# The end of a two-layer attention kernel: another division, norms by halves, two stores

## The chip, the cores and the metric

The kernel runs on one core of one Trainium2 chip. A core has a matrix engine (TensorE, PE in the profile), a vector engine (VectorE, DVE), a scalar engine (ScalarE, ACT), a general engine (GpSimd, POOL) and SyncE (SP), which here issues all transfers (DMAs). Each engine takes its instructions strictly in the order in which the program issues them to it, and engines wait for each other by semaphores. On-chip memory (SBUF) has 128 partitions, which are the rows of a tile; TensorE writes to a small memory of its own (PSUM). DRAM lies outside.

The metric is the device time in microseconds (us) of one execution; less is better.

## What is computed

Two layers of attention over x of 2048 rows and 256 columns, with 16 heads of 16 columns each. Layer 0 modulates, attends within and across the two halves of x, and ends with a GELU MLP. Layer 1 is cut below to what matters here; `memory` is a context of 1601 rows.

```python
def _layernorm(x, g, b):
    mu = jnp.mean(x, axis=-1, keepdims=True)
    var = jnp.var(x, axis=-1, keepdims=True)
    return (x - mu) * jax.lax.rsqrt(var + EPS) * g + b

x = tgt + _mha(tgt, tgt, tgt, ..., tgt_mask)      # stage 2, masked
x = _layernorm(x, g1, be1)
x = x + _mha(x, memory, memory, ..., None)        # stage 3
x = _layernorm(x, g2, be2)
x = x + (jax.nn.relu(x @ w1 + b1) @ w2 + b2)
x = _layernorm(x, g3, be3)
```

Within `_mha` the softmax over keys is followed by the product with the values, and the heads' outputs, side by side, by the projection `out @ ow + ob`.

## The kernel before

The 2048 rows are cut into four blocks of 512 (`BLK`), the 16 heads into four groups of four. A *unit* is one block and one group in one of four attention stages (0 and 1 of layer 0, 2 and 3 of layer 1). `stream` (L1197) runs all units one after another. For a unit TensorE makes the scores (L1035, L1042, masked ones L1050 too), ScalarE their exponentials (L1055), TensorE the product with the values into `u["av"]` (L1072). The scores of the next unit are made once more beforehand (L957) for their maxima. Between these steps the rest of the work is woven in by hand: generators in `background` that `advance` moves one step at a time, and `later`, a list of functions with a due step. A generator is a *chain*: what one block needs after its last group, namely projection, norm, MLP, and the next stage's queries, keys and values. Because the schedule is manual, the order in the program is the order on each engine.

A value matrix carries a column of ones, so that `u["av"]` holds for each head of the group, on 32 partitions each, 16 rows of sums and one row with the sum of the weights (row `ONE` = 16). The division of a unit is three functions:

- `copy_sums` (L1091): ScalarE copies `u["av"]` to `sums` (L1104). Four DMAs (L1110) spread the four rows of weights as 128x16 over all partitions, `weights`. Four more (L1119) bring the sums to the block's tile `oT`, where the heads lie without gaps: 64 rows for a group.
- `invert` (L1133): VectorE's reciprocal of the 128x16 weights (L1136). `to_rows` writes it to DRAM (L1141) and fetches it from there, each head's row copied to 16 partitions (L1143), into `rd_rows`.
- `divide` (L1146): GpSimd multiplies the 64x512 rows of `oT` by `rd_rows` (L1150).

For all units but the last, `invert` comes 3 and `divide` 6 steps after `copy_sums`, beside the next unit. After the last unit nothing is left to stand beside: `stream` runs what is pending, then the three functions in a row (L1336 to L1339), and then the last block's chain to its end.

That chain is `chain_last` (L745):

- `residual` loads t, the block's rows so far, 128x4x256 (L180). The tile has one buffer.
- `project` (L498) multiplies `oT` by the output weights in two halves of two row tiles each (L507); 256 columns of a tile are one row tile. `biased` (L530) takes each half: VectorE adds the bias row into u (L537), GpSimd adds u to t (L539).
- `post_norm` (L543): `normalize` runs VectorE's bn_stats (L366) and bn_aggr (L369) for all four row tiles, adds eps (L371), GpSimd raises to -1/2 (L372), VectorE applies mean and factor to each row tile (L375). GpSimd then multiplies by the row g and adds the row b, in two halves each, 128x512 (L550).
- `transposed` (L381): TensorE turns t (L390) by columns: all four row tiles of the first 128 columns, then of the second. ScalarE copies the first to `hT` (L405), VectorE the second (L407).
- `mlp` (L553): eight products up (L565) with ReLU on ScalarE (L574), then down in two halves (L618), each given to `biased` again.
- `post_norm` again, and one DMA of the block to `out` (L755).

A step that fills a PSUM bank is a `piece` (L118); its later functions, such as the copy out of the bank, are run when the chain moves on. SP's queue holds in its last part the division's DMAs, then the load of t, then the store.

Of the kernel before, what the change touches and what calls it, by code (L numbers as in the profile page):

```python
# [12 lines left out]
F32 = mybir.dt.float32  # L13
# [3 lines left out]
AF = mybir.ActivationFunctionType  # L17
ALU = mybir.AluOpType
# [4 lines left out]
P = 128  # L23
D = 256
H = 16
HD = 16
# [4 lines left out]
BLK = 512  # L31
NB = S // BLK
TPB = BLK // P
# [4 lines left out]
PH = 32  # L38
ONE = HD
# [37 lines left out]
def two_layers(ctx: ExitStack, tc: tile.TileContext, a: dict, out: bass.AP):  # L77
    nc = tc.nc

    def pool(name, bufs=1, **kw):  # L80
        return ctx.enter_context(tc.tile_pool(name=name, bufs=bufs, **kw))
# [7 lines left out]
    sb = pool("sb")  # L89
# [28 lines left out]
    def piece(*steps):  # L118

        yield BANK  # L120
        if streaming[0]:
            n = small[0]
            m = one_ps(n=n)
        else:
            n = None
            while len([e for e in unfinished if e[0] is None]) > 2:
                flush_one()
            m = ps.tile([P, 2, BLK], F32, tag="s", bufs=3, name="s_ps")[:, 0, :]
        left = [lambda f=f: f(m) for f in steps[1:]]
        entry = (n, left)  # L130
        unfinished.append(entry)
        steps[0](m)
        while left:

            yield 1 if len(left) > 1 else 0
            if left:
                left.pop(0)()
        if entry in unfinished:
            unfinished.remove(entry)

    def flush_one():
# [37 lines left out]
    def load_x(t, src):  # L179
        nc.sync.dma_start(t, src)  # L180
# [4 lines left out]
    def along(row, n=TPB, parts=P):  # L185
        return row.unsqueeze(1).to_broadcast([parts, n, D])
# [4 lines left out]
    def half(shape, dtype=F32, name="half"):  # L191
        return sb.tile(shape, dtype, tag="half", bufs=3, name=name)
# [76 lines left out]
    for g in range(NG):  # L269
        for i in range(2):  # L270
            at = (2 * g + i) * HD
# [19 lines left out]
    m = one_ps()  # L291
# [40 lines left out]
    m = one_ps()  # L332
# [165 lines left out]
    def project(st, b, finish):  # L498

        oT, wp = blocks[st, b]["oT"], outputs[st]  # L500

        def product(m, n):
            y = m.rearrange("p (t d) -> p t d", d=D)
            for q2 in range(2):
                qt = 2 * n + q2
                for k in range(2):
                    nc.tensor.matmul(  # L507
                        y[:, q2, :], lhsT=oT[:, k, qt * P : (qt + 1) * P],
                        rhs=wp[:, k, :], start=k == 0, stop=k == 1,
                    )  # L510

        for n in range(2):
            yield from piece(
                lambda m, n=n: product(m, n),
                lambda m, n=n: finish(n, m.rearrange("p (t d) -> p t d", d=D)),
            )
        done.add(("project", st, b))
# [111 lines left out]
    def residual(src):  # L629
        t = sb.tile([P, TPB, D], F32, tag="t", name="t")  # L630
        load_x(t, src)
        return t
# [112 lines left out]
    def chain_last(b):  # L745
# [8 lines left out]
        yield from post_norm(rows["m1"], t)  # L754
        nc.sync.dma_start(out[b * BLK : (b + 1) * BLK, :].rearrange("(t p) d -> p t d", p=P), t)  # L755

    chains = (chain_self, chain_cross, chain_masked, chain_last)
    blocks: dict = {}
    background: list = []
# [19 lines left out]
    def ensure(what):  # L779

        while what not in done:
            if not advance(background[0]):
                background.pop(0)
# [7 lines left out]
    def want(*place):  # L791
        waiting.extend((kind, *place) for kind in ("keys", "values"))
# [225 lines left out]
    def part_tile(u, name):  # L1018
        return sb.tile([P, 4 * BLK // P], F32, tag=f"{name}{u['g']}{u['part']}", name=name)
# [71 lines left out]
    def copy_sums(u):  # L1091


        st, b, g = u["st"], u["b"], u["g"]
        first_part = u.get("part") == 0
        if g == 0 and not first_part:
            before = ORDER[st].index(b)
            if before:
                ensure(("project", st, ORDER[st][before - 1]))
            elif st:  # L1100
                ensure(("project", st - 1, ORDER[st - 1][-1]))
            blocks[st, b]["oT"] = sb.tile([P, 2, BLK], F32, tag="oT", name="oT")
        sums = half([P, BLK], name="sums")
        nc.scalar.copy(sums, u["av"])  # L1104
        if "part" in u:
            u["weights"] = part_tile(u, "weights")
        else:
            u["weights"] = sb.tile([P, 4 * BLK // P], F32, tag="rd", bufs=4, name="weights")
        for j in range(4):
            nc.sync.dma_start(  # L1110
                u["weights"][PH * j : PH * (j + 1), :], sums[PH * j + ONE : PH * j + ONE + 1, :]
            )
        at = (g % 2) * (P // 2)
        if first_part:
            dst = first_sums[g] = dr.tile([P // 2, BLK], F32, tag="o", bufs=NG, name="o_dr")
        else:
            dst = blocks[st, b]["oT"][at : at + P // 2, g // 2, :]
        for j in range(4):
            nc.sync.dma_start(dst[HD * j : HD * (j + 1), :], sums[PH * j : PH * j + HD, :])  # L1119

        if st < 3 and b in (ORDER[st][-1], ORDER[st][1]):
            for slot in u["slots"]:
                if (st == 1 and slot == 1 and g in (1, 2)) or (st == 2 and b != ORDER[st][-1]):
                    continue
                want(st + 1, g, slot)
        if st == 1 and b == ORDER[1][-1] and g == 1:
            mask_part(0)
        if first_part and g == NG - 1:
            want(2, 2, 1)
# [3 lines left out]
    def invert(u):  # L1133

        rd = sb.tile([P, 4 * BLK // P], F32, tag="rd", bufs=4, name="rd")
        nc.vector.reciprocal(rd, u["weights"])  # L1136
        u["rd"] = to_rows(u, rd, sb.tile([P, BLK], F32, tag="rd_rows", name="rd_rows"))

    def to_rows(u, rd, dst):
        d = dr.tile([4, BLK], F32, tag="rd", bufs=4, name="rd_dr")  # L1140
        nc.sync.dma_start(d.rearrange("j (p c) -> (j p) c", p=PH), rd)  # L1141
        at = (u["g"] % 2) * (P // 2)
        nc.sync.dma_start(dst[at : at + P // 2, :], d.unsqueeze(1).to_broadcast([4, HD, BLK]))  # L1143
        return dst[at : at + P // 2, :]

    def divide(u):  # L1146
        g = u["g"]
        at = (g % 2) * (P // 2)
        v = blocks[u["st"], u["b"]]["oT"][at : at + P // 2, g // 2, :]
        nc.gpsimd.tensor_tensor(v, v, u["rd"], ALU.mult)  # L1150
        if u.get("part") == 1:
            rows_, sums = u["rd_first"], u["first"]
            nc.gpsimd.tensor_tensor(sums, sums, rows_, ALU.mult)
            nc.gpsimd.tensor_tensor(v, v, sums, ALU.add)
# [24 lines left out]
    def fetch_first(u):  # L1179
# [4 lines left out]
        nc.sync.dma_start(t[at : at + P // 2, :], first_sums[u["g"]])  # L1184
        u["first"] = t[at : at + P // 2, :]

    def chain_after(u):

        go = now[0] + (9 if "part" in u else 8)

        def gen():
            yield max(0, go - now[0])
            yield from chains[u["st"]](u["b"])

        background.append([gen(), 0, False])

    def stream(stages):  # L1197

        units = []
# [16 lines left out]
        at = 0  # L1216
# [69 lines left out]
        for u in units:  # L1286
            i = u["i"]
# [3 lines left out]
            for s2 in range(len(second)):  # L1291
# [22 lines left out]
                if s2 == 2 and i:  # L1314
                    w = units[i - 1]
# [10 lines left out]
                    if w["g"] == NG - 1 and part != 0:  # L1326
                        chain_after(w)
        small[0] = len(units) % 2
        for f in pending:
            if f:  # L1330
                f()
# [1 line left out]
            x[1]()  # L1333
        flush((0, 1))
        streaming[0] = False
        w = units[-1]  # L1336
        copy_sums(w)
        invert(w)
        divide(w)  # L1339
        chain_after(w)  # L1340
        while background:
            if not advance(background[0]):
                background.pop(0)
# [109 lines left out]
```

## Time and profile before

| | us |
|---|---|
| median of 3 runs | 3333.31 |
| lowest and highest run | 3326.55, 3346.01 |
| the profiled execution, its time | 3340.76 |
| its span, first to last instruction | 3338.9 |
| busy in the span: PE | 3054.3 |
| DVE | 2164.9 |
| ACT | 1718.1 |
| POOL | 404.0 |
| mean granted clock of PE | 0.969 |

The profile is of one execution, not of a median one: what is worked out from its rows stands against 3340.76. The profile has a page and can be asked for views. In the page, the span is cut into 40 slices with a digit for the busy tenths of each engine. The chain of waits starts at the last instruction and goes back: each piece is what released the next. "PE s_ps L507 x14" is 14 TensorE instructions of line 507 that write `s_ps`; "SPq" and "POOLq" are the engine's own queue work; "DMA rd_rows<-rd_dr" is the time from a transfer's issue until it was seen to have landed. In the timeline a row gives start, duration, engine, line, operation, shapes, and in brackets how long the engine had been idle and what ended that. A granted clock of 1.00 is full speed of PE, 0.50 half.

A product in 32 bits is two instructions on PE, so the eight products of `project`, four for each half, are the 16 instructions of L507.

### The profile page before, as it was taken

The page shows a single profiled execution, that of the slowest core. Times are in us where ns is not written, and L with a number is a line of the kernel's source. Part 1 is how long each engine was busy: PE and PEld are TensorE (multiplying, and loading weights), DVE is VectorE, ACT ScalarE, POOL GpSimd, SP SyncE. Part 2 cuts the span into 40 slices and gives each one's busy share as a digit, 9 for nine tenths or more (in the row PEclk, how much of TensorE's full clock was granted, in tenths as well). Part 3 has the DMA queues.
Part 4 walks back from the last instruction along what each step waited for, and adds up shares of the span by engine and source line. Part 5 has one row for each costly group of instructions (what it writes and reads, how often), then busy time and mean ns, then how long its engine had stood idle before and what let it go on. Part 6 is the DMA issues. An engine that isn't in the chain of part 4 may idle for free.

```text
span 3338.9 us, 56839 instructions
## 1 busy us (share of the span) xinstructions
PE 3054.3 (91%) x22592; PEld 1371.8 (41%) x22592; DVE 2164.9 (65%) x3925; ACT 1718.1 (51%) x1892; POOL 404.0 (12%) x344
## 2 busy tenths in 40 slices
PE   5889999999998989898999999999989999999995
PEld 2434444444444435343433343343344444444433
DVE  4666777775656566566777777777667757666541
ACT  1455565565555545443545555555556546545461
POOL 0001101101011122113013013010010010110102
PEclk8899999999999999999999999999999999999997
DMA  6462251260216121343012011003230100001000
GB/s 171 131 118 80 63 98 58 72 114 26 66 33 116 31 79 42 95 117 101 27 39 59 20 39 52 13 22 70 49 87 27 27 17 21 26 17 27 11 14 16
DMA packets 162363, 191.21 MB, mean 57 GB/s; under 512 B 82584, under 2 KB 95520, under 8 KB 162096
## 3 DMA queue, kind: packets, MB, share of 16 engines
q1 hardware_dynamic: 162096, 187.57, 22.8%
q8 instruction: 178, 2.92, 0.4%
q14 instruction: 89, 0.73, 0.1%
HBM read 129.91 MB, written 48.46 MB: 53 GB/s over the span
## 4 chain that ended last, share of the span: by engine, by line
PE 59%; DVE 6%; ACT 4%; DMA 3%; SPq 2%; issue 2%; POOL 1%; ACTq 0%; POOLq 0%; DVEq 0%
PE m_ps L1072 15%; PE s_ps L1035 10%; PE s_ps L957 9%; PE s_ps L1050 7%; PE s_ps L1042 6%; ACT e L1055 3%; PE m_ps L565 3%; PE m_ps L618 3%; DVE s_ps L965 2%; DVE pm L972 1%; PE m_ps L507 1%; PE m_ps L432 1%; DMA kT<-k_dr 1%; PE m_ps L462 1%; DVE t L375 1%
## 5 line engine op out<-in xcount | busy, mean ns | idle before, releaser
L1055 ACT ACTIVATE e<-s_ps 128x1024 f32<-128x1024 f32 (+1 forms) x1440 | 1466.9, 1024 | 1330.7 <-PE s_ps L1042 739.4
L972 DVE TENSOR_REDUCE pm<-s_ps 128x2 f32<-128x1024 f32 (+3 forms) x1024 | 1122.5, 1107 | 512.2 <-PE s_ps L957 508.9
L1072 PE MATMUL m_ps<-e,V 128*32 128x256 f32 (+2 forms) x10432 | 909.7, 420 | 1.0 <-DVE lo L440 0.8
L965 DVE CUSTOM_DVE_ANT_0 s_ps<-s_ps,bias 128x512 f32<-128x512 f32 x1024 | 713.2, 701 | 286.7 <-PE s_ps L957 147.4
L957 PE MATMUL s_ps<-kT,q 64*128 64x512 f32 (+3 forms) x3072 | 655.5, 428 | 112.4 <-ACT e L1055 63.9
L1035 PE MATMUL s_ps<-q,kT 64*128 64x512 f32 (+1 forms) x2880 | 681.6, 469 | 45.0 <-ACT e L1055 24.7
L1042 PE MATMUL s_ps<-nm,sel 64*128 64x512 f32 (+1 forms) x2880 | 576.2, 395 | 0.0
L957 PEld LDWEIGHTS s_ps<-kT,q 64*128 64x128 f32 x3072 | 295.4, 187 | 475.2 <-issue 244.1
L1035 PEld LDWEIGHTS s_ps<-q,kT 64*128 64x128 f32 (+1 forms) x2880 | 271.5, 185 | 506.9 <-issue 286.6
L1072 PEld LDWEIGHTS m_ps<-e,V 128*32 128x32 f32 (+1 forms) x10432 | 207.2, 109 | 442.6 <-issue 420.7
L1050 PE MATMUL s_ps<-biasT,ident 128*128 128x512 bf16 x1024 | 311.0, 385 | 0.0
L1150 POOL TENSOR_TENSOR oT<-oT,rd_rows 64x512 f32<-64x512 f32 x64 | 81.6, 1275 | 1873.6 <-DMA rd_rows<-rd_dr 1540.2
L1042 PEld LDWEIGHTS s_ps<-nm,sel 64*128 64x128 f32 (+1 forms) x2880 | 277.0, 188 | 10.3 <-ACT nm L1001 0.5
L902 POOL TENSOR_SCALAR bias<-raw 128x512 bf16<-128x512 int32 x64 | 123.0, 1923 | 275.5 <-DMA raw<-in_mask 264.1
L965 DVE DVE_READ_ACCUMULATOR2_ANT pm<- 128x1 f32 x1024 | 145.3, 142 | 0.0
L1050 PEld LDWEIGHTS <-ident 128*128 128x128 bf16 x1024 | 58.3, 97 | 186.4 <-issue 186.4
L432 PE MATMUL m_ps<-hT,w_qk 128*128 128x512 f32 (+2 forms) x224 | 106.6, 599 | 10.4 <-DVE lo L440 7.7
L565 PE MATMUL m_ps<-hT,w_mlp 128*128 128x512 f32 x224 | 110.4, 616 | 5.7 <-ACT sums L1104 4.4
L440 DVE SCALAR_TENSOR_TENSOR lo<-m_ps,qkb,hi 128x512 fp32r<-128x512 f32 (+2 forms) x56 | 41.1, 734 | 109.7 <-ACT hi L439 66.0
L618 PE MATMUL m_ps<-w_mlp,hid 128*128 128x256 f32 x448 | 104.6, 387 | 0.0
L618 PEld LDWEIGHTS m_ps<-w_mlp,hid 128*128 128x128 f32 x448 | 83.9, 191 | 19.3 <-issue 8.5
L462 PE MATMUL m_ps<-w_v,hT 128*128 128x256 f32 (+1 forms) x244 | 63.8, 407 | 25.6 <-DVE lo L440 22.6
(107 smaller groups left out, 1278.0 us busy)
## 6 DMA issues: line engine op xcount, KB each, us to landing
q<-q_dr SPq DMA_DIRECT2D x544, 64.0 KB
kT<-k_dr SPq DMA_DIRECT2D x192, 128.0 KB
raw<-in_mask SPq DMA_DIRECT2D x64, 256.0 KB
q_dr<-hi SPq DMA_DIRECT2D x32, 256.0 KB
q_dr<-lo SPq DMA_DIRECT2D x32, 256.0 KB
oT<-sums SPq DMA_DIRECT2D x256, 32.0 KB
rd_rows<-rd_dr SPq DMA_DIRECT2D x64, 128.0 KB
v_dr<-v SPq DMA_DIRECT2D x14, 544.0 KB
```

The costliest lines, as they stand in the source:

```text
L432: nc.tensor.matmul(m[:, :n], lhsT=wqk[:, k, w, c, :], rhs=hT[:, k, :n], start=k == 0, stop=k == 1)
L565: nc.tensor.matmul(m, lhsT=w1[k][:, f * P : (f + 1) * P], rhs=hT[:, k, :], start=k == 0, stop=k == 1,)
L618: nc.tensor.matmul(m[:, q2 * D : (q2 + 1) * D], lhsT=hid[f][:, qt * P : (qt + 1) * P], rhs=w2[f // 4][:, f % 4, :], start=f == 0, stop=f = ...
L902: nc.gpsimd.tensor_scalar(bias_rows[b, slot, qt][:, j * BLK : (j + 1) * BLK], raw, 0.0, MASKED, ALU.is_equal, ALU.mult,)
L957: nc.tensor.matmul(s[:, h, :nn], lhsT=u["q"][64 * h : 64 * h + 64, i, qt * P : (qt + 1) * P], rhs=kT[g][slot][64 * h : 64 * h + 64, i, c : ...
L965: nc.vector.tensor_tensor_reduce(out=s[:, h, :], in0=s[:, h, :], in1=bias_rows[b, slot, qt][:, c : c + nn], scale=1.0, scalar=-3.0e38, op0 ...
L972: nc.vector.tensor_reduce(u["pm"][:, qt, :, i, n], s[:, :, :nn], AX.X, ALU.max)
L1035: nc.tensor.matmul(s[:r, h, :], lhsT=kT[g][slot][64 * h : 64 * h + 64, i, kt * P : kt * P + r], rhs=u["q"][64 * h : 64 * h + 64, i, :], st ...
L1042: nc.tensor.matmul(s[:r, h, :], lhsT=sel[64 * h : 64 * h + 64, i, :r], rhs=u["nm"][64 * h : 64 * h + 64, :], start=False, stop=not masked,)
L1050: nc.tensor.matmul(s[:, h, :], lhsT=ident16, rhs=bias_columns[b, slot, kt], start=False, stop=True,)
L1055: nc.scalar.activation(e[:r], s[:r], AF.Exp, scale=SCALE)
L1072: nc.tensor.matmul(u["av"][PH * j : PH * (j + 1), cut], lhsT=V[g][slot][:r, kt * GW + j * VW : kt * GW + j * VW + PH], rhs=u["e"][n, j % 2 ...
```

## The change

Only the end of `stream` and what it calls are edited. The last unit no longer goes through `copy_sums`, `invert`, `divide` and `chain_last` but through `end_sums` and `chain_end`. The load of t stands ahead of the last pending value products.

`end_sums`: ScalarE copies the sums as before. Four DMAs take each head's row of weights straight from `sums` to the 16 partitions of its head in `rd_rows`. Four DMAs bring the sums to `oT` as before. VectorE takes the reciprocal of 64x256 and multiplies `oT` by it, first for the first 256 rows of the block, then for the others.

`chain_end`: each half of the projection is added and normed for itself. `added` puts both sums on VectorE. `norm_half` does a norm for two row tiles; of it only the power stays on GpSimd, with 128x2; g and b go into two VectorE operations for each row tile, (t - mean) * g and then * factor + b. The transposes go by halves of rows, four into one bank, and ScalarE copies each half of `hT`. The MLP is the same function; its results are added and normed by halves, and each half is stored by a DMA of its own.

```diff
+    def norm_half(r, t, n):
+        mv = sb.tile([P, TPB, 2], F32, tag="mv", bufs=2, name="mv")
...
+        two = range(2 * n, 2 * n + 2)
+        for i in two:
+            nc.vector.bn_stats(st[:, i, :], t[:, i, :])
+        for i in two:
+            nc.vector.bn_aggr(mv[:, i, :], st[:, i, :])
+        cut = slice(2 * n, 2 * n + 2)
+        nc.vector.tensor_scalar(ve[:, cut], mv[:, cut, 1], 1e-5, None, ALU.add)
+        nc.gpsimd.tensor_tensor(rs[:, cut], ve[:, cut], minus_half[:, cut], ALU.pow)
+        for x, op, y in ((mv[:, :, 0], ALU.subtract, 1), (rs, ALU.mult, 2)):
+            for i in two:
+                nc.vector.scalar_tensor_tensor(
+                    t[:, i, :], t[:, i, :], x[:, i : i + 1], r[:, y, :], op,
+                    ALU.mult if y == 1 else ALU.add,
+                )
+
+    def added(r, t, n, y):
+        u = half([P, 2, D], name="u")
+        th = t[:, 2 * n : 2 * n + 2, :]
+        nc.vector.tensor_tensor(u, y, along(r[:, 0, :], 2), ALU.add)
+        nc.vector.tensor_tensor(th, th, u, ALU.add)
+
+    def chain_end(b):
+        t = last_t[0]
+        def project_half(n, y):
+            added(rows["a3"], t, n, y)
+            norm_half(rows["a3"], t, n)
+        yield from project(3, b, project_half)
+        hT = sb.tile([P, 2, BLK], F32, tag="hT", name="hT")
+        x = BLK // 2
+        for n in range(2):
+            def turn(m, n=n):
+                for k in range(2):
+                    for i in range(2):
+                        at = k * x + i * P
+                        nc.tensor.transpose(
+                            m[:, at : at + P], t[:, 2 * n + i, k * P : (k + 1) * P], ident
+                        )
+            def take(m, n=n):
+                nc.scalar.copy(
+                    hT[:, :, n * x : (n + 1) * x], m.rearrange("p (k x) -> p k x", k=2)
+                )
+            yield from piece(turn, take)
+        def result_half(n, y):
+            added(rows["m1"], t, n, y)
+            norm_half(rows["m1"], t, n)
+            at = b * BLK + n * x
+            nc.sync.dma_start(
+                out[at : at + x, :].rearrange("(t p) d -> p t d", p=P), t[:, 2 * n : 2 * n + 2, :]
+            )
+        yield from mlp(mlp1[0], 8, AF.Relu, hT, result_half)
...
+    def end_sums(u):
+        g = u["g"]
+        at = (g % 2) * (P // 2)
+        rows_ = slice(at, at + P // 2)
+        sums = half([P, BLK], name="sums")
+        nc.scalar.copy(sums, u["av"])
+        oT = blocks[u["st"], u["b"]]["oT"][rows_, g // 2, :]
+        rd = sb.tile([P, BLK], F32, tag="rd_rows", name="rd_rows")
+        for j in range(4):
+            r = slice(at + HD * j, at + HD * (j + 1))
+            row = sums[PH * j + ONE : PH * j + ONE + 1, :]
+            nc.sync.dma_start(rd[r, :], row.unsqueeze(1).to_broadcast([1, HD, BLK]))
+        for j in range(4):
+            nc.sync.dma_start(oT[HD * j : HD * (j + 1), :], sums[PH * j : PH * j + HD, :])
+        for n in range(2):
+            cut = slice(n * (BLK // 2), (n + 1) * (BLK // 2))
+            nc.vector.reciprocal(rd[rows_, cut], rd[rows_, cut])
+            nc.vector.tensor_tensor(oT[:, cut], oT[:, cut], rd[rows_, cut], ALU.mult)
...
         small[0] = len(units) % 2
+        last_t.append(residual(xs[3, units[-1]["b"]]))
         for f in pending:
             if f:
                 f()
...
         streaming[0] = False
-        w = units[-1]
-        copy_sums(w)
-        invert(w)
-        divide(w)
-        chain_after(w)
+        end_sums(units[-1])
+        background.append([chain_end(units[-1]["b"]), 0, False])
```

More of the change, by code (lines that the diff above doesn't have):

```diff
@@ L755, in chain_last @@
         nc.sync.dma_start(out[b * BLK : (b + 1) * BLK, :].rearrange("(t p) d -> p t d", p=P), t)
+    def norm_half(r, t, n):
+        mv = sb.tile([P, TPB, 2], F32, tag="mv", bufs=2, name="mv")
+        rs = sb.tile([P, TPB], F32, tag="rs", bufs=2, name="rs")
+        st = sb.tile([P, TPB, 6], F32, tag="bn", bufs=2, name="bn")
+        ve = sb.tile([P, TPB], F32, tag="ve", bufs=2, name="ve")
+        two = range(2 * n, 2 * n + 2)
[12 more added lines that the diff above has]
+                )
@@ L757, in two_layers @@
+    last_t: list = []
     chains = (chain_self, chain_cross, chain_masked, chain_last)
```

## The prediction

> **What bounds the kernel now.** The page comes first. Its slices show TensorE busy at 90% and more nearly throughout, and at half in the last slice:
>
> ```profile
> PE   5889999999998989898999999999989999999995
> POOL 0001101101011122113013013010010010110102
> PEclk8899999999999999999999999999999999999997
> ```
>
> A slice is 83.5 us, and no other slice holds code that the diff changes: up to the last attention unit the instructions stay the same and in the same order. So the change acts on what comes after the last unit. A table of two stretches, 33 us before the unit's end and 76 us after it, says how different they are (columns: stretch, us, busy us and count for TensorE, its weight loads, VectorE, ScalarE, GpSimd, then granted clock, DMA share, GB/s):
>
> ```profile
> 3230.00:3263.00 33.00, 32.83 (x294) 11.80 (x290) 0.25 (x1) 26.10 (x27) 1.28 (x1) 1.00 0.04 10
> 3263.00:3339.00 76.00, 38.22 (x120) 24.82 (x118) 11.15 (x32) 6.44 (x10) 18.32 (x15) 0.74 0.06 18
> ```
>
> TensorE is full in the first and works for half of the second. There the chain of waits, in order of time, names each step (start, us, what):
>
> ```profile
> 3262.77 0.59 ACT sums L1104
> ...
> 3268.44 1.59 DMA rd_dr<-rd
> ...
> 3270.08 4.69 DMA rd_rows<-rd_dr
> ...
> 3275.02 1.27 POOL oT L1150
> ...
> 3276.34 5.92 PE s_ps L507 x14
> ...
> 3289.23 3.71 POOL t L550 x3
> ...
> 3294.52 15.98 PE s_ps L565 x32
> 3310.51 13.83 PE s_ps L618 x64
> ...
> 3331.33 2.48 POOL t L550 x2
> 3333.81 1.22 POOLq L1449
> ```
>
> The reader is to see four stretches: the division (sums copied, to 3276.34, when the projection starts), projection with the first norm (to 3294.3), the MLP (to 3324.3), the last norm with the store (to 3338.9). The change touches all but the third. Single durations come from the timeline (start, us, engine, line):
>
> ```profile
> 3267.15 0.25 DVE L1136 RECIPROCAL rd<-weights 128x16 f32<-128x16 f32 x1 [30.27 <-DMA weights<-sums]
> ...
> 3285.72 1.02 POOL L372 TENSOR_TENSOR rs<-ve,minus_half 128x4 f32<-128x4 f32 x1 [1.35 <-DVE ve L371]
> 3286.77 1.38 DVE L375 TENSOR_SCALAR t<-t,mv,rs 128x256 f32<-128x256 f32 x4 [1.13 <-POOL rs L372]
> ...
> 3335.05 0.39 SPq L755 DMA_DIRECT2D out<-t  x1
> ```
>
> **Part A, the division.** Before, from the first SP issue (3263.38) to the projection takes 12.96 us: eight issues at 0.63 each, the write of the inverse to DRAM (1.59), its fetch to rows (4.69), GpSimd's product (1.27) and gaps. After, the eight issues stay: four row broadcasts in the place of the four weight loads (32 KB each for 2 KB), then the same four loads of oT, the last of which ends its issue at 3268.34. The two DRAM hops and GpSimd go. The weight loads had landed 1.34 after their last issue ended (3265.81 to 3267.15); with that, oT is there at 3269.7, and the broadcasts, ahead of them in the queue, at 3267.2. Their reciprocal of 64x256 fits between, if it takes under 2.5.
>
> The trace has no reciprocal of that size. From below it is bounded by any 128x256 operation of VectorE (0.41), from above by the 128x16 row scaled: 0.247 against 0.172 for other 128x16 operations is 4.7 ns more per column, so 0.41 + 256 x 0.0047 = 1.6. I take 1.6, as the row is of the same operation. [...]
>
> Then a product of 64x256 (0.41, as the 128x256 rows) and 0.1 of hand-over: the projection starts at 3270.2, so **6.1 us** are saved. Bounds: a broadcast may take as long as the 128 KB fetch (4.69 from its issue, thus 3269.9, then 1.6, 0.41 and 0.1: 3272.0, saving 4.3); or the oT loads land 0.5 sooner (6.6). The second half's 1.6 + 0.41 lie beside the projection's first half (six matmuls at 0.42, 2.5); without that cover they would cost 2.0.
>
> The load of t moves ahead of the unit's end. It is one 512 KB transfer, and it passes eight issues and the two hops on SP's queue; SP is idle from 3240.2 to 3263.4 and the earlier store of t (issued at 3177.5) is long done, so it waits for nothing and lies beside attention: 0 us. Without that cover it would cost its 0.45 of issue and its traffic. It also leaves the stretch where it lay beside the fetch to rows.
>
> **Part B, projection and first norm.** Before, 18.0 us from projection to MLP (3276.34 to 3294.34). After, with S for the projection's start: the first half's sums are there at S+3.03, as before (3279.37). Each half on VectorE is u 0.70, sum into t 0.70 (GpSimd 1.27 before), two bn_stats 0.75, two bn_aggr 0.20, ve 0.20, hand-over 0.07, GpSimd's power, hand-over 0.03, four operations with scale and shift 1.40 (as the four in 1.38 above), gaps 0.10: 4.15 plus the power. The power is 1.02 for 4 columns. For 2 columns it is not in the trace: at most 1.02, at least 0.51 in proportion. GpSimd's plain 128x512 product takes 1.27, so fixed cost is small there and I take 0.51. A half is 4.66.
>
> VectorE waits for the power, and behind that wait stand the second half's u and all of its norm, so the halves run one after another: S+3.03+2x4.66 = S+12.35. The second half's matmuls (done at S+6) are hidden in this. Four transposes 1.15 (six took 1.54), copy 0.59 and hand-overs 0.13 follow: MLP at S+14.2, **3.8 us** saved; with the power at 1.02 it is 2.8. The first half's transposes and copy lie beside the second half's norm. GpSimd's four products with rows (4.99) are gone, and with them DVE's stall beside them.
>
> **Part C, the MLP** is unedited: 30 us, 0. Its first stretch runs at a granted clock of 0.50 (to 3298.7), which an earlier start can shift; this is a rival below.
>
> **Part D, last norm and store.** Before, 14.54 from the last u (3324.36) to the end: 10.69 to the store's issue, 3.85 after. After: the first half's norm (4.66) lies beside the second half's matmuls (6.85, from 3317.51 to 3324.36), its store too; if it were longer than 6.85 the excess would be added. The second half needs 4.7 to its issue: 6.0 saved. The store moves 256 KB instead of 512, which had moved in 1.53 (3336 to 3337.6 at 338 GB/s): 0.77 saved, and the fixed rest of 2.3 stays. **6.8 us**, with the power at 1.02 it is 6.3. One more issue of 0.39 on SP, beside matmuls.
>
> **The sum.** 6.1 + 3.8 + 6.8 = 16.7, and against the profiled execution 3340.76 (span 3338.9 and 1.9 around it) that gives 3324.0. That execution lies 7.4 above the median of the runs shown (3333.31; 3326.55 to 3346.01). The tail's cost doesn't depend on where the rest fell, so the forecast is 3333.3 - 16.7 = **3316.6**. Both ends of each bound: saving 4.3 + 2.8 + 6.3 = 13.4 to 6.6 + 3.8 + 6.8 = 17.2.
>
> **The rivals.**
>
> One, *the small gain*: the broadcasts land late and the power is all fixed cost, saving 13.4, thus 3319.9. For it: all 32 KB of each broadcast come out of a single partition, which no transfer of this size in the trace does. Against it: there are 0.9 us of slack before oT's landing (3267.2 + 1.6 against 3269.7).
>
> Two, *TensorE's clock falls otherwise*. Rows of 1 us show the granted clock at 0.50 from 3264.6, 1.00 from 3281.7, 0.50 from 3285.1 and 1.00 again from 3298.7: steps at multiples of 3.41. The MLP began 4.4 before the last of them, and its matmuls took 0.85 each until then and 0.43 after. A shorter idle time before it could leave it warm at once (0.5 x 4.4 = 2.2 more saved, 18.9, 3314.4); a start just after a step could cost nearly two steps (6.8 slow, 1.2 lost, 15.5 saved, 3317.8). [...]
>
> Three, *slower*: one partition feeds a broadcast no faster than it fed a weight load. If all of the 1.34 went into reading 2 KB, 32 KB take 16 x 1.34 = 21.4; the four side by side land at 3287.2, the projection starts at 3289.3, 13.0 later than before, against 10.6 saved in B and D: 2.4 slower, 3335.7; one after another it is 64 us more, 3399.9. It decides from a landing 18.9 us after the issue (3265.8 + 18.9 + 2.1 = 3286.8, 10.5 late). Against it: the oT loads, 2 KB rows out of 16 partitions, moved 62 and 43 KB in 1 us each, at the rate at which they were issued.
>
> Four, *that it doesn't do what it says*: t's early load waits, or halves wait for whole tiles. Then the first half's transposes and store move behind the second half: 0.4 and 0.8 lost. That the projection's first two matmuls start at 3262.59 while the third waits for the division shows that parts of oT are tracked apart. It is counted with the small gain.
>
> **How the numbers follow.** Forecast 0.55, small gain 0.27, clock 0.14 (both ways), slower 0.04. A measurement of this kernel can tell about 0.5%, 16.7 us, from no change, and the forecast lies on that bound. The median of few runs moves by some 5 us of itself (the three shown span 19.5), so the forecast's share goes to both sides, somewhat more to faster as B is costed with full gaps: 0.32 of 0.55; of the small gain 0.11, of the clock 0.11. Faster 0.54, same 0.43, slower 0.03 (serial broadcasts, half of rival three, and a drift). The range takes 13.4 to 18.9 and twice that 5 us: 3305 to 3329. The forecast's own is 3310 to 3323.
>
> **What will show it.** Right: from the last copy of sums to the projection's restart some 7.4 us instead of 13.6; reciprocals of 64x256 of 1.6 each, the first ended before oT's product starts; the power at half of 1.02; from the last u to the end 7.8 instead of 14.5; no GpSimd work but the power. Wrong: a broadcast whose wait ends last in the division, two reciprocals ahead of the projection, or an MLP stretch longer than 30 us.

## The result, and the profile after

The change made the kernel 16.9 us faster: a median of 3318.44 us (3310.87 to 3326.87, 8 runs) against 3335.36 for the kernel before (3326.55 to 3346.65, 8 runs), a ratio of 0.995 with a 95% interval of 0.9934 to 0.9965. The profiled execution took 3326.87 us, with a span of 3325.1.

In the page after, the last slice has changed, while the other slices differ by a tenth here and there:

```profile
PE   5889999999998989898999999999999999999997
POOL 0001101101010121204013012100010011110110
PEclk8899999999999999999999999999999999999998
```

The table of two stretches, cut where the last unit ends, shows the end 17 us shorter, with VectorE busy for 20.9 us of it instead of 11.2 and GpSimd for 3.3 instead of 18.3. TensorE has the same work, at a granted clock of 0.83 instead of 0.74:

```profile
3233.00:3266.00 33.00, 32.83 (x293) 11.85 (x292) 0.25 (x1) 25.97 (x27) 1.27 (x1) 1.00 0.09 26
3266.00:3325.00 59.00, 37.09 (x120) 23.79 (x119) 20.91 (x48) 7.18 (x11) 3.26 (x4) 0.83 0.08 14
```

The chain of waits of the kernel after, over the same end (start, us, what):

```profile
3265.91 0.59 ACT sums L1260
...
3270.30 1.66 DMA oT<-sums
3271.97 0.01 issue
3271.98 1.76 DVE rd_rows L1271
3273.74 0.02 issue
3273.76 0.43 DVE oT L1272
3274.20 0.09 issue
3274.29 2.91 PE s_ps L507 x6
...
3285.29 0.50 DVE t L773
...
3285.92 1.22 PE s_ps L802 x4
...
3287.80 15.80 PE s_ps L565 x32
3303.60 13.83 PE s_ps L618 x64
...
3321.05 0.48 DVE t L773
```

Both hops through DRAM, GpSimd's product and its work on rows are gone. One reciprocal stands ahead of the projection, as foreseen; but it begins 6.07 behind the copy's start, and the piece ahead of it names a load of oT, on which it doesn't depend.

In what follows the *end* of a kernel is the time from the start of the last copy of sums to the end of the span in its one profile, and it is cut where the projection resumes, the MLP's first product starts and the last u starts. The end is a better measure of these edits than whole times: the instructions up to the copy, the same in all kernels but for a load and two small copies, took between 3248.8 and 3272.9 us in the profiles of this study, while the last norm and store took 7.45 to 7.67 in all eight profiles that have it as after, and the division 8.32 to 8.39 in all six. Only the stretches of TensorE's own work vary more (the MLP 27.85 to 30.91), with its clock.

| us | division | projection, norm | MLP | norm, store | end |
|---|---|---|---|---|---|
| before | 13.57 | 18.00 | 30.02 | 14.54 | 76.13 |
| after | 8.38 | 13.51 | 29.65 | 7.65 | 59.19 |
| e1_division | 8.36 | 17.15 | 29.57 | 14.64 | 69.72 |
| e2_norms | 12.45 | 13.59 | 30.91 | 7.45 | 64.40 |
| e12_early_t | 12.45 | 18.27 | 30.14 | 14.50 | 75.36 |
| e3_one_store | 8.36 | 13.51 | 29.64 | 8.43 | 59.94 |
| e8_whole | 8.39 | 13.58 | 30.03 | 10.86 | 62.86 |
| e6_power_first | 8.32 | 16.14 | 30.11 | 8.87 | 63.44 |
| e4_act_queue | 8.82 | 13.52 | 29.54 | 7.66 | 59.54 |
| e5_sixteen_sources | 7.61 | 13.52 | 30.51 | 7.67 | 59.31 |
| e7_products | 4.78 | 13.29 | 29.83 | 7.64 | 55.54 |
| e9_banks | 3.56 | 12.59 | 29.28 | 7.67 | 53.10 |
| e10_warm | 8.35 | 12.22 | 27.85 | 7.61 | 56.03 |
| e11_both | 3.55 | 12.23 | 27.85 | 7.63 | 51.26 |

The change's saving of 16.94 is thus 5.19 in the division, 4.49 in projection and norm, 0.37 in the MLP, 6.89 in the last norm and store.

### The profile page after: what moved, and what is told of

It is laid out like the page before. It is cut to its first block, busy times and chain, and to the rows that moved or that the text cites. A ratio compares the mean times of both kernels' runs of the same rounds, so it can differ in the third digit from the quotient of the medians.

```text
span 3325.1 us, 56840 instructions
## 1 busy us (share of the span) xinstructions
PE 3054.1 (92%) x22592; PEld 1369.6 (41%) x22592; DVE 2175.1 (65%) x3941; ACT 1720.0 (52%) x1893; POOL 389.1 (12%) x333
## 2 busy tenths in 40 slices
DMA packets 162103, 191.20 MB, mean 58 GB/s; under 512 B 82324, under 2 KB 95260, under 8 KB 161836
## 4 chain that ended last, share of the span: by engine, by line
PE 60%; DVE 6%; ACT 4%; DMA 3%; SPq 2%; issue 2%; POOL 1%; ACTq 0%; DVEq 0%; POOLq 0%
PE m_ps L1139 16%; PE s_ps L1102 10%; PE s_ps L1024 9%; PE s_ps L1117 7%; PE s_ps L1109 6%; ACT e L1122 4%; PE m_ps L565 3%; PE m_ps L618 3%; DVE s_ps L1032 2%; DVE pm L1039 1%; PE m_ps L507 1%; PE m_ps L432 1%; PE m_ps L462 1%; DVE t L375 1%; POOL bias L969 1%
## 5 line engine op out<-in xcount | busy, mean ns | idle before, releaser
L1117 PEld LDWEIGHTS <-ident 128*128 128x128 bf16 x1024 | 58.3, 97 | 186.8 <-issue 186.8
```

The lines of the kernel that those rows point to most:

```text
L1117: nc.tensor.matmul(s[:, h, :], lhsT=ident16, rhs=bias_columns[b, slot, kt], start=False, stop=True,)
```

## The experiments

### Do the parts add up?

**e1_division** keeps `end_sums` and goes on with the old chain.

```diff
-        last_t.append(residual(xs[3, units[-1]["b"]]))
...
         end_sums(units[-1])
-        background.append([chain_end(units[-1]["b"]), 0, False])
+        chain_after(units[-1])
```

> The division of the change alone; norms, transposes and store as before. The end (from the last copy of sums to the end of the span) was 76.1 us before and 59.2 after. Theory, the parts add: from the copy to the projection 8.4 as after, the rest as before, an end of 76.1 - 5.2 = 70.9. Rival, the parts hide each other (the early load of t or the halves on VectorE are needed for the division to pay): the division takes 10 or more, an end above 72.5.

**e2_norms** keeps `chain_end` behind the old division.

```diff
-        end_sums(units[-1])
+        w = units[-1]
+        copy_sums(w)
+        invert(w)
+        divide(w)
         background.append([chain_end(units[-1]["b"]), 0, False])
```

> The division as before (two hops through DRAM, GpSimd's product), norms by halves and two stores as after. Theory, the parts add: 13.6 to the projection, then 13.5 to the MLP, 29.7 in it and 7.7 after, an end of 64.4. As the load of t no longer lies beside the fetch to rows, that fetch takes 3.8 to 4.0 instead of 4.69, an end of 63.6. Rival, the halves pay only behind a division by halves: 15 or more to the MLP, an end above 66.

The ends were 69.72 and 64.40, both on the theory's side: each part pays without the other. e1's end is 1.2 below its 70.9, because its projection and its MLP took 0.85 and 0.45 less than before. By rows of 1 us the granted clock was back at full speed 3.6 us behind the start of the projection in e1, and 5.3 us behind it in before; half of the difference is the 0.85. That e2 meets 64.4 is chance: its division took 1.1 less than the theory had, and its MLP 1.2 more, as the clock stayed at 0.50 for 6.2 us of it (3.7 in after).

The savings, 6.41 and 11.73, are 18.1 together, 1.2 more than the change. In e2's chain of waits the fetch is shorter than the 4.69 of before:

```profile
3268.97 1.63 DMA rd_dr<-rd
3270.65 3.63 DMA rd_rows<-rd_dr
```

**e12_early_t** is the kernel before with the early load of t alone.

```diff
+        last_t.append(residual(xs[3, units[-1]["b"]]))
...
-        t = residual(xs[3, b])
+        t = last_t.pop() if last_t else residual(xs[3, b])
```

> The kernel before with one edit: t is loaded ahead of the last value products, as in the change. Theory, the division alone (end 69.7) and the norms alone (64.4) save 18.1 together where the change saves 16.9, because both count what the early or later load of t gives: it no longer lies beside the fetch to rows. Then this edit alone shortens that fetch from 4.69 to 3.6 and the end from 76.1 to 75.0 (74.5 to 75.5 with what TensorE's clock does in the MLP). Rival, the 1.2 are chance of the clock: the fetch stays at 4.5 or more, an end of 75.6 to 76.6.

The end was 75.36 and the fetch took 3.62:

```profile
3259.11 1.62 DMA rd_dr<-rd
3260.79 3.62 DMA rd_rows<-rd_dr
...
3264.57 1.27 POOL oT L1151
```

So 1.12 of the division's 5.19 (13.57 to 12.45) could have been had by moving one load, without the new division: 512 KB no longer share the DMA engines with the transfer that the division waits for (in half-microsecond rows their busy share reaches 1.02 in before's fetch, 3272.5 to 3273.0 at 315 GB/s, and 0.21 in the fetch of the unit ahead of it, 3241.0 to 3242.5, which has no such load beside it). The end kept 0.77 of it, as the projection took 0.27 and the MLP 0.12 longer. The new division itself is worth 4.07 (12.45 to 8.38). In e1 and e2 the 1.1 is counted twice, as e1's division is as short as after's without the early load (8.36). That is nearly all of the 1.2; what else the two differ by in projection and MLP cancels (0.77 more, 0.81 less).

### What holds the reciprocal?

**e4_act_queue** issues the four oT loads from ScalarE's queue.

```diff
-            nc.sync.dma_start(oT[HD * j : HD * (j + 1), :], sums[PH * j : PH * j + HD, :])
+            nc.scalar.dma_start(oT[HD * j : HD * (j + 1), :], sums[PH * j : PH * j + HD, :])
```

> As after, but the four loads of oT are issued by ScalarE's queue, beside SyncE's four broadcasts. After, the reciprocal began 2.97 us behind the end of the last broadcast's issue, and the profile names an oT load as what it waited for. Theory, the broadcasts are slow because all 16 rows of one are read from one partition: the reciprocal begins no sooner than 2.7 behind that issue (later, if the oT loads share the way), and the projection begins 8.0 to 9.0 behind the copy. Rival, the reciprocal waits for oT loads as the row says: these are issued 2.5 sooner, the reciprocal begins 1.4 behind the last broadcast's issue, the projection some 6.8 behind the copy.

The issues ran side by side, and the reciprocal began later, not sooner: 6.51 behind the copy, 3.42 behind the last broadcast's issue. The timelines, after first:

```profile
3266.57 2.42 SPq L1266 DMA_DIRECT2D rd_rows<-sums  x4
3269.04 2.48 SPq L1268 DMA_DIRECT2D oT<-sums  x4
3271.98 1.75 DVE L1271 RECIPROCAL rd_rows<-rd_rows 64x256 f32<-64x256 f32 x1 [31.96 <-DMA oT<-sums]
```

```profile
3270.98 2.77 ACTq L1268 DMA_DIRECT2D oT<-sums  x4
3271.03 2.42 SPq L1266 DMA_DIRECT2D rd_rows<-sums  x4
3276.87 1.75 DVE L1271 RECIPROCAL rd_rows<-rd_rows 64x256 f32<-64x256 f32 x1 [32.35 <-DMA oT<-sums]
```

The bracket again names oT. Its loads were issued 2.5 us sooner relative to the copy, and the reciprocal began 0.44 later, so they are hardly what ended the wait: the releaser in the bracket is inferred. The next run settles it.

**e5_sixteen_sources** gives each transfer 16 source partitions.

```diff
-            row = sums[PH * j + ONE : PH * j + ONE + 1, :]
-            nc.sync.dma_start(rd[r, :], row.unsqueeze(1).to_broadcast([1, HD, BLK]))
+            nc.sync.dma_start(rd[r, :], sums[PH * j : PH * j + HD, :])
```

> As after, but each of the four transfers into rd_rows takes 16 rows from 16 partitions of the sums instead of one row 16 times (so the sums are divided by other sums: this leaves out the broadcast of the weights). Bytes, destinations, queue and number of issues are the same. Theory, reading one partition is what makes the broadcast slow: these transfers land as weight loads do, 1.34 us behind the last issue, the reciprocal begins 4.4 behind the copy instead of 6.07, the oT loads (last issue ends at 5.6, landing 1.34 later) now end the wait, the projection begins at 7.5, an end of 58.3. Rival, 32 KB take that long from anywhere: the reciprocal begins at 6.0 as after, an end of 59.2.

The reciprocal began at 4.56, while the oT loads were still being issued (to 3267.29), so it doesn't wait for them, and the bracket was wrong before. It is now attributed to its own transfers, and the oT loads end the next wait:

```profile
3262.35 2.41 SPq L1265 DMA_DIRECT2D rd_rows<-sums  x4
3264.81 2.48 SPq L1267 DMA_DIRECT2D oT<-sums  x4
3266.25 1.75 DVE L1270 RECIPROCAL rd_rows<-rd_rows 64x256 f32<-64x256 f32 x1 [30.27 <-DMA rd_rows<-sums]
3268.77 0.42 DVE L1271 TENSOR_TENSOR oT<-oT,rd_rows 64x256 f32<-64x256 f32 x1 [0.78 <-DMA oT<-sums]
```

The projection resumed at 7.61, as the theory had it (7.5). The end was 59.31 and not 58.3, because the MLP took 30.51: the clock stayed at 0.50 for 5.4 us of it (3.7 in after). It meets the rival's 59.2 by this chance; the reciprocal's start, 4.56 and not 6.0, decides. So a broadcast is slow because it reads one row 16 times; the packets of these transfers have the same number and size in both kernels (the page counts 162103 packets and 191.20 MB in each, with 82324 under 512 B and 95260 under 2 KB). In the kernel after, half-microsecond rows show it (the last columns are granted clock, DMA share, GB/s); the first lies in the broadcasts, the second in the oT loads:

```profile
3268.50:3269.00 0.50, 0.00 (x0) 0.00 (x0) 0.00 (x0) 0.00 (x0) 0.00 (x0) 0.50 1.04 37
...
3271.00:3271.50 0.50, 0.00 (x0) 0.00 (x0) 0.00 (x0) 0.00 (x0) 0.00 (x0) 0.50 0.31 99
```

The DMA engines are all busy for 37 GB/s in one, and a third busy for 99 GB/s in the other. The rates were 25 to 37 GB/s at first (3267.5 to 3269.5) and 57 to 62 later (to 3270.5); why a row read 16 times is slow, and why the rate then rose, no run here shows.

### What do the halves and the order of the norm give?

**e3_one_store** stores the result by one transfer of 512 KB.

```diff
-            at = b * BLK + n * x
-            nc.sync.dma_start(
-                out[at : at + x, :].rearrange("(t p) d -> p t d", p=P), t[:, 2 * n : 2 * n + 2, :]
-            )
+            if n == 1:
+                nc.sync.dma_start(
+                    out[b * BLK : (b + 1) * BLK, :].rearrange("(t p) d -> p t d", p=P), t
+                )
```

> As after, but the result is stored by one transfer of 512 KB when the second half is normed. Theory: the smaller last transfer is worth what 256 KB take at 338 GB/s, 0.8, an end of 60.0. Rival: the end is fixed waiting after the issue, and the store by halves is worth under 0.2, an end of 59.2 to 59.4.

The end was 59.94: the store by halves is worth 0.75.

**e8_whole** does each norm for four row tiles at once behind the second half (`norm_whole`, the operations of `norm_half` for all four), with one store. The same edit is made for the MLP's result.

```diff
             added(rows["a3"], t, n, y)
-            norm_half(rows["a3"], t, n)
+            if n == 1:
+                norm_whole(rows["a3"], t)
```

> As after, but the norms are done for all four row tiles at once behind the second half (VectorE alone, the same operations), and the result is stored by one transfer; the division and the transposes by halves stay. Theory, in the first norm the halves save little, as the second half's chain stands last either way: MLP 0.9 later; in the last norm they hide a whole half beside the matmuls: 2.9 longer, and 0.8 for the store, an end of 63.8. Rival, what pays is only that GpSimd's 128x512 operations are gone, and halves are worth under 1 in all: an end below 60.2.

The first norm took 13.58 against 13.51: halves are worth nothing there. The two half chains run one after another on VectorE, and the second starts when the first lets it, not when its products are done. The whole norm starts later, but takes 5.03 from its first bn_stats to its end, where two halves take 3.04 each; in both kernels the norm ends 11.88 behind the projection's start. The last norm took 10.86 against 7.65, and 0.75 of these 3.2 is the store: there the first half hides beside 6.8 us of matmuls. The theory was near in the last norm (2.9 expected without the store, 2.5 found) and not in the first (0.9 expected, 0.07 found).

**e6_power_first** does a half's norm in the order of before.

```diff
-        for x, op, y in ((mv[:, :, 0], ALU.subtract, 1), (rs, ALU.mult, 2)):
-            for i in two:
-                nc.vector.scalar_tensor_tensor(
-                    t[:, i, :], t[:, i, :], x[:, i : i + 1], r[:, y, :], op,
-                    ALU.mult if y == 1 else ALU.add,
-                )
+        for i in two:
+            nc.vector.tensor_scalar(
+                t[:, i, :], t[:, i, :], mv[:, i, 0:1], rs[:, i : i + 1], ALU.subtract, ALU.mult
+            )
+        th = t[:, 2 * n : 2 * n + 2, :]
+        for y, op in ((1, ALU.mult), (2, ALU.add)):
+            nc.vector.tensor_tensor(th, th, along(r[:, y, :], 2), op)
```

> As after, but the norm of a half subtracts the mean and multiplies by the factor in one operation for each row tile (as before), then multiplies by g and adds b with 128x512 operations on VectorE. Theory, after gained 0.7 more than forecast in the first norm because its pass with the mean doesn't need the power, which hides the power's 0.82: here the power is waited for, a half takes 5.8 from u to u instead of 4.49, the MLP begins 2.6 later, the last norm takes 1.3 longer, an end of 63.1. Rival, the gain came from elsewhere (TensorE's clock in the projection) and the power costs nothing in any order: the two more columns' passes alone, 2 x 0.41 + 2 x 0.70 against 4 x 0.44, cost 0.5 a half, an end of 60.6.

The MLP began 2.6 later and the last norm took 1.22 longer, an end of 63.44, as the theory had it (63.1). The timelines, e6 first, show why:

```profile
3272.76 0.71 POOL L770 TENSOR_TENSOR rs<-ve,minus_half 128x2 f32<-128x2 f32 x1 [31.75 <-DVE ve L769]
3273.50 0.73 DVE L772 TENSOR_SCALAR t<-t,mv,rs 128x256 f32<-128x256 f32 x2 [0.89 <-POOL rs L770]
```

```profile
3279.82 0.87 DVE L773 SCALAR_TENSOR_TENSOR t<-t,mv,rows 128x256 f32<-128x256 f32 x2
3280.06 0.81 POOL L770 TENSOR_TENSOR rs<-ve,minus_half 128x2 f32<-128x2 f32 x1 [31.55 <-DVE ve L769]
3280.90 0.88 DVE L773 SCALAR_TENSOR_TENSOR t<-t,rs,rows 128x256 f32<-128x256 f32 x2 [0.20 <-POOL rs L770]
```

In e6 VectorE stands idle for 0.89 while GpSimd raises to the power. In the kernel after, the pass with the mean and g runs in that time, and VectorE waits 0.20. From u to u a half takes 5.62 in e6 and 4.41 in the kernel after; 0.7 of the difference is this wait, and 0.4 the passes, 2.15 (0.73 and 1.42) against 1.75.

### What bounds the new end?

**e7_products** needs no transfer. `picks` are columns of the identity, copied ahead of the end: for each head its weight's column 16 times, and its 16 columns of sums.

```diff
+        for cut in cuts:
+            nc.scalar.copy(sums[:, cut], u["av"][:, cut])
+        for cut in cuts:
+            for k in range(2):
+                nc.tensor.matmul(
+                    m[rows_, k, cut], lhsT=picks[0][:, k, :], rhs=sums[:, cut],
+                    start=True, stop=True,
+                )
+        for cut in cuts:
+            nc.vector.reciprocal(rd[rows_, cut], m[rows_, 0, cut])
+            nc.vector.tensor_tensor(oT[:, cut], m[rows_, 1, cut], rd[rows_, cut], ALU.mult)
```

> As after, but no transfer in the division: two products on TensorE with columns of the identity, each by halves of 256 columns, bring the weights to the 16 rows of each head and the sums to their place in PSUM, from where VectorE takes the reciprocal and the product into oT; ScalarE copies the sums by halves. Theory, what is left of the division is issue and landing of transfers (5.4 of 8.38 ahead of the reciprocal): the reciprocal begins 1.1 to 1.6 behind the copy, the projection at 3.5 to 4.2, an end of 54.3 to 55.1. Rival, the products run at half clock and reading PSUM slows VectorE: the projection at 5 or later, an end above 55.8.

The projection resumed at 4.78 and the end was 55.54, between theory and rival. The reciprocal began at 2.46, 0.09 behind the end of the last of the four products, though it needs only the first:

```profile
3249.19 1.94 PE L1268 MATMUL s_ps<-sums,picks 128*64 128x256 f32 x8 [0.48 <-ACT sums L1265]
3251.22 1.76 DVE L1273 RECIPROCAL rd_rows<-s_ps 64x256 f32<-64x256 f32 x1 [28.16 <-PE s_ps L1268]
```

**e9_banks** gives the products tiles of their own (the cut stands against e7).

```diff
-        m = ps.tile([P, 2, BLK], F32, tag="s", bufs=3, name="s_ps")
+        def two():
+            return ps.tile([P, 2, BLK], F32, tag="s", bufs=3, name="s_ps")
+        first, m0, m1 = one_ps(), two()[:, 0, :], two()
+        places = ((first, m0), (m1[:, 0, :], m1[:, 1, :]))
```

> As e7_products, but the first half's weights, the first half's sums and the second half each have a PSUM tile of their own; in e7 all four products wrote one tile, and the first reciprocal began only when the last product was done, 2.46 behind the copy's start. Theory: with a tile of its own it begins behind the first product, at 1.1 to 1.3, the projection at 3.4 to 3.7, an end of 54.2. Rival, the reciprocal is held by something else, the slow stretch of the products: it begins at 2.4, an end of 55.5.

`places` puts the first half's weights into `first`, its sums into `m0`, and both of the second half into the two halves of `m1`. The reciprocal began at 1.17 and the projection at 3.56:

```profile
3272.90 0.65 ACT L1269 COPY sums<-m_ps 128x256 f32<-128x256 f32 x2 [1.17 <-PE m_ps L1139]
3273.33 0.65 PE L1272 MATMUL m_ps<-sums,picks 128*64 128x256 f32 x2 [0.48 <-ACT sums L1269]
3274.07 1.76 DVE L1277 RECIPROCAL rd_rows<-m_ps 64x256 f32<-64x256 f32 x1 [26.86 <-PE m_ps L1272]
3275.93 0.43 DVE L1278 TENSOR_TENSOR oT<-s_ps,rd_rows 64x256 f32<-64x256 f32 x1
```

Half of what is left of the division is the reciprocal. The end, 53.10, is 1.1 below the 54.2 expected: with a shorter gap TensorE was at full clock in the projection, and that stretch took 12.59 (13.51 in after); the MLP took 0.37 less.

**e10_warm** is the kernel after with throwaway products in TensorE's gaps.

```diff
+    def warm(n):
+        m = one_ps()
+        for _ in range(n):
+            nc.tensor.matmul(
+                m, lhsT=identR, rhs=negpad.rearrange("p t x -> p (t x)"), start=True, stop=True
+            )
...
         end_sums(units[-1])
+        warm(28)
...
         yield from project(3, b, project_half)
+        warm(9)
...
             yield from piece(turn, take)
+            warm((14, 2)[n])
```

> As after, with throwaway products of 128x512 on TensorE in its gaps: 28 behind the last value products, 9 behind the projection, 14 between the two halves' transposes, 2 ahead of the MLP; nothing reads them. Theory, the granted clock falls to 0.50 because TensorE stands idle: it now stays at 1.00, the first half of the projection takes 1.5 instead of 2.9, the MLP 27.9 to 28.3 instead of 29.65, the transposes 0.5 less, an end of 55.5 to 56.2. Rival, the clock falls whatever is done there, or the throwaway products hold up the true ones by as much: an end of 58.5 or more.

The granted clock stayed at 1.00, the MLP took 27.85 and projection and norm 12.22, an end of 56.03, as the theory had it. A stretch of its end, and such a stretch in the kernel after:

```profile
3270.00:3283.00 13.00, 11.59 (x50) 9.03 (x49) 7.19 (x13) 0.15 (x1) 0.26 (x1) 1.00 0.22 20
```

```profile
3267.00:3279.00 12.00, 4.71 (x14) 3.79 (x14) 5.90 (x7) 0.00 (x0) 0.00 (x0) 0.57 0.24 22
```

The clock is 1.00 in the first and 0.57 in the second. So 3.2 us of the end of the kernel after (59.19 to 56.03) are TensorE at half clock because it stood idle.

The first half of the projection took 2.05 to its u, and not 1.5. At full clock it no longer covers the second half's reciprocal and product: u stands behind them on VectorE and starts 0.03 after they end (3279.94 and 3279.97). e9 shows the same (3278.50 and 3278.53). So in both it is VectorE, and not TensorE, that the first norm's start waits for.

**e11_both** joins e9 and the last three of e10's four groups.

> e9_banks with the throwaway products of e10_warm behind the projection, between the transposes and ahead of the MLP (none in the division, where TensorE already stands idle for under 1.5). Theory, the two add where they don't meet: the division of e9 (3.56), the rest of e10 (47.7 from the projection), an end of 51.2, 24.9 less than before, so a ratio of 0.9925 to before, against 0.995 of the change. Rival, the clock falls in another place or the gains of e10 lie in its longer division: an end of 52.5 or more, a ratio of 0.993 or above.

The end was 51.26, the sum of the two where they don't meet. Over 6 runs the median was 3318.01 against 3337.0 for before, a ratio of 0.9937 (0.9918 to 0.9955). By the end the theory holds. The whole times don't decide: the theory's ratio (0.9925) lies in the interval, but so does the rival's (0.993 or above), on whose side the median's ratio is, and the interval overlaps that of the change. The 7.9 us between the ends of e11 and after are seen in one profile of each, not in whole times, which spread over 12 to 20 us.

## Why the prediction was right

The forecast saving was 16.7; the end became 16.94 shorter and the median 16.9. The mechanism held: the two hops through DRAM, GpSimd's work on rows and half of the last norm no longer stand in the chain. That the sum was right to 0.2 is luck: its errors had both signs, 0.9 too much in the division, 0.7 and 0.4 too little in the first norm and the MLP, and the interval of the whole times alone is 12 to 22 us saved. One of the signs of being wrong that the prediction named came true, a broadcast whose wait ends last in the division, and one of being right didn't, the power at half of 1.02.

**Part A, 6.1 forecast, 5.19 measured: too much by 0.9.** The step that failed is "the weight loads had landed 1.34 after their last issue ended ...; with that, ... the broadcasts, ahead of them in the queue, at 3267.2". The broadcasts landed 2.97 behind their last issue (3269.00 to 3271.97). The 0.9 of slack that the forecast had was used up, and the reciprocal, not the oT loads, set the projection's start. With 16 source partitions (e5) the landing was 1.49 behind, near the forecast's 1.34, so the cause is shown as far as the one source row; why such a row is slow is not. The bound of the prediction (4.69 from the issue) held it (3.56), as did its first rival, in the place if not in the amount. The third rival, 21 us for a broadcast, fell.

The reciprocal was forecast at 1.6 from the 16-column row, meant as a bound from above, and took 1.75; (1.75 - 0.247) / 240 columns is 6.3 ns a column. That the second half's reciprocal lies beside the projection was right.

The early load of t was costed at nothing, with "it also leaves the stretch where it lay beside the fetch to rows" and no price for that. Here it changes no sum, as the fetch is gone (e1's division takes 8.36 without it); by e12 it was worth 1.1 in the old division.

**Part B, 3.8 forecast, 4.49 measured: too little by 0.7.** The step that failed is "VectorE waits for the power". It holds only for the second pass: the first needs the mean alone and runs beside the power, so that a wait of 0.20 is left where the forecast put 0.61 into the chain, the power with its hand-overs. Two sizes erred the other way. The power of two columns was taken as 0.51, in proportion; it took 0.81 and 0.86, and 0.70 to 0.71 without VectorE beside it (e6), so some 0.4 of it does not grow with the columns (1.02 for four). The four operations with scale and shift were put at 1.40, as the four of L375, which read one tile; with a row as their second input they took 1.75 (0.87 and 0.88). In all, a half took 4.41 from u to u and not 4.66. e6, which has the order that the forecast assumed, took 5.62: with that order part B would have saved 1.9 (18.00 to 16.14).

And the last transposes begin when the first row tile of the half is ready, not when both are (3285.92, while the last operation of the norm ran to 3286.17), which the sum of whole durations missed.

That the halves run one after another on VectorE was right; e8 adds that they gain nothing there.

**Part C, 0 forecast, 0.37 measured,** within what the clock does: in the profiles with no throwaway products the MLP took 29.28 to 30.91. The second rival had 27.8 to 31.2 (2.2 less to 1.2 more), and both the spread and its cause, e10, bear it out; it didn't decide.

**Part D, 6.8 forecast, 6.89 measured.** The first half's norm lay beside the second half's products, and the smaller store was worth 0.75 (0.77 forecast).

The fourth rival fell: halves of oT and of t were waited for apart. The projection resumed at 3274.29, while the second half's reciprocal ran, and the first half's transposes (3281.53) lay beside the second half's norm. That tiles are not always so was met in e7, where the first reciprocal waited for products into other columns and the other half of its PSUM tile (2.46 behind the copy, against 1.17 in e9 with tiles apart).

## What to carry to other kernels

A transfer that reads one partition's row many times is not priced by a load of the same size: here four such transfers landed 2.97 us behind their last issue where loads from 16 partitions landed 1.49 behind (e5), and a product with columns of the identity had half of the columns spread in 0.74 (e9, 3273.33 to 3274.07). When a norm must wait for a power or another engine's scalar, put ahead of it the pass that doesn't need it: here VectorE waited 0.20 with that pass ahead, and 0.89 without (e6). Halves pay where the first half lies beside other engines' work, as in the last norm (2.5 without the store, e8), and not where one engine does both in a row, as in the first (0.07).

## What the runs showed that was not expected

GpSimd's power is slower beside VectorE's two-input passes: 0.70 to 0.71 alone against 0.79 to 0.87 for 128x2, and 1.12 to 1.17 (e8) against 1.02 for 128x4. So the runs show 0.1 to 0.16 more on GpSimd and none on VectorE, whose two passes take 0.87 beside the power and 0.88 behind it.

The steps of the granted clock lay about a multiple of 3.41 apart in before (17.1, 3.4 and 13.6) and after (10.2, 6.8 and 6.9) alike. By rows of 1 us it fell at 3267.6 in the kernel after, rose at 3277.8, fell at 3284.6 and rose at 3291.5, so the MLP began at half clock again, 3.7 us ahead of the next step (4.4 before).

What moves the start of the end by up to 24 us from execution to execution, with nearly the same instructions ahead of it, stays open.
